# delta * u on GpSimd in three chunks, side additions one slot later, in_proj's input two blocks ahead, and the last image worked in parallel parts

## The chip, the cores and the metric

The kernel runs on one core of one Trainium2 chip. The time is device microseconds of one execution; the time before is the median of three executions. Engines are named as in the profile: PE (TensorE, matrix products and transposes), DVE (VectorE), ACT (ScalarE), POOL (GpSimd) and SP (SyncE, which here issues every DMA).

## The reference, cut to what matters

Four images of 64 x 64 positions and 96 channels pass a stack of layers. Layer 0 is a two-dimensional state-space block: a group norm, an input projection, a depthwise 3 x 3 convolution with SiLU, four selective scans (rows, columns, and both backwards), their merge, a layer norm, a gate and an output projection. Layer 1 is the same kind of block with 384 inner channels, between a real 2D Fourier transform and its inverse. Layers 2 and 3 are an attention without softmax, so that it can be done with small matrices, and a feed-forward part in quantised numbers. Everything but these quantised products is float32.

```python
def _selective_scan(u, dts, A, Bs, Cs, Dskip, delta_bias):
    delta = jax.nn.softplus(dts + delta_bias[None, :, :, None])
    ...
    def step(hst, inputs):
        ul, dl, bl, cl = inputs
        dA = jnp.exp(dl[..., None] * A)
        hst = hst * dA + (dl * ul)[..., None] * bl[:, :, None, :]
        y = jnp.einsum('bkdn,bkn->bkd', hst, cl)
        return (hst, y)
    ...
    return ys + Dskip[None, :, :, None] * u
...
x = x + _L0_conv_ref(_gn(x), ...)
x = _L1_conv_ref(x, ...)
t = _to_tokens(x)
t = t + _L2_attn_ref(_ln_t(t), ...)
t = t + _L2_ffn_ref(_ln_t(t), ...)
t = t + _L3_attn_ref(_ln_t(t), ...)
t = t + _L3_ffn_ref(_ln_t(t), ...)
```

The product `dl * ul` is the `du` of this document. The state has 16 entries for each channel.

## The kernel before, in words

**Three parts.** `build` first prepares image pair 0 alone (the head), then runs `scans` (the loop), then finishes image 3 alone (the tail). In head and tail a task owns the engines, with `wide=4` and eight PSUM buffers. In the loop the order on PE, DVE, ACT and POOL is written by hand and followed as it stands.

**The loop.** It has six phases: two image pairs of layer 0 (64 channels of both images side by side, three chunks of 128 partitions) and four images of layer 1. A phase is four directions, each cut into segments: eight of 512 positions in layer 0, and 512, 512, 384, 384 and 320 in layer 1. A segment is 12 steps: the state's entries in four groups `q` of four, and for each group the three channel chunks `c`. There are 144 segments and 1728 steps. A step on DVE is two scans `hx` (entries 4q and 4q+1), two scans `hy`, and the product `hcy` = hy * C. On POOL it is `hcx` = hx * C, a copy of the last state (`keep_state`, only where a segment isn't the last of its direction), and then, for the step that follows, `front_b`: two products hy = du * B. For `hx`, the input term comes from PE (transposes of `bx`) into PSUM instead. ACT makes the decays (`exp` in `front_x` and `front_y`) and `bx`; PE sums the products over the state in PSUM (`accumulate`). There is one buffer of `hy`: `front_b` of a step overwrites what `hcy` of the step before reads.

**The next segment.** While a segment is scanned, `prepare` makes what the next one needs, a piece at each slot: x_proj (`xpw`), dt (`dtw`), the softplus in one burst on ACT, `du` = delta * u (one DVE instruction over all three chunks, in a slot of the kind LATE), the load of u for the segment after (`load_u`, one buffer), and the transposed `dut`. At step 9 (`c == 0` of the last group) what is left of it is drained.

**Side work.** The other layers' work stands in lists of generators, one list for each phase. A step has three slots: after the two hx scans, after the first hy scan, and (LATE) ahead of `hcy`. At each, `prepare` advances, and a side task advances when a budget, `rate / 3` for each slot, has grown to one. A task's instructions up to its next `yield` are put there. `E.defer` holds an instruction until the next advance. All side work shares one PSUM buffer (`ms`). `E.require` runs a task to its end where a segment needs its result. The lists that matter here are `begin0` and `begin1` (norm or Fourier, in_proj by `visits`, convolution), `gate`, `end0` (`gated` with `out0`) and `end1` (`gated` with `out1`, then `inverse` and `tokens`).

**The tail** runs `end1` for image 3: `gated` (each block of up to 8 columns: the four directions' outputs and u are loaded by twos, summed by transposes on PE, normed with two products by `mean_w`, scaled, gated and projected), `inverse` (32 channels at a time) and `tokens` (layer norm over all 32 tiles in turn, the small products, attention group by group, norm, feed-forward group by group; two layers). Each of these runs as one stream.

Of the kernel before, what the change touches and what calls it, by code (L numbers as in the profile page):

```python
# [6 lines left out]
F32 = mybir.dt.float32  # L7
# [18 lines left out]
RATES = [1.75, 2.25, 2.35, 2.35, 2.35, 2.35]  # L26
# [97 lines left out]
class Block:  # L124
# [59 lines left out]
    def visits(self, E, sp, wi, xf, blocks, half, nm, w, done):  # L184


        def load(r, n):
            x = sp.tile([CH, 2, 512], F32, name=f"xi{half}_{nm}_{r}", tag=f"xin{w}", bufs=2)
            self.nc.sync.dma_start(out=x[:, :, : n * 64], in_=xf[:, :, r * 64 : (r + n) * 64])
            return x  # L190

        nxt = load(*blocks[0])
        yield
        yield
        for b, (r, n) in enumerate(blocks):
            x, nxt = nxt, load(*blocks[b + 1]) if b + 1 < len(blocks) else None
            pi = E.psum(f"pi{half}_{nm}_{r}")
            yield from self.in_proj(pi, wi, half, x, n * 64)
            E.defer(lambda r=r, n=n, pi=pi: done(r, n, pi))
            yield  # L200
# [149 lines left out]
    def gated(self, E, g, io, out_proj):  # L350


        nc, cfg = self.nc, self.cfg
        yn, yo = io["y"][cfg.nat], io["y"][1 - cfg.nat].rearrange("k (w r) c -> r w k c", r=cfg.NR)
        u, gz = io["u"][cfg.nat], io["gz"]
        with E.pool(f"{cfg.pre}nm{g}") as sp:
# [3 lines left out]
            tiles = [  # L360
                (b, i, r + i, min(2, n - i)) for b, (r, n) in enumerate(cfg.rows) for i in range(0, n, 2)
            ]

            def load(b, i, r, n):
                nm = f"{cfg.pre}_{g}_{r}"
                yt = sp.tile([P, 2, 2, C * P], F32, name=f"yt_{nm}", tag="yt", bufs=2)
# [5 lines left out]
                ut = sp.tile([P, C, P], F32, name=f"ut_{nm}", tag="ut", bufs=2)  # L372
# [3 lines left out]
            todo = iter(tiles)  # L376
            nxt = load(*next(todo))
            yield
            yield
            yield  # L380
            for b, (r, nr) in enumerate(cfg.rows):
                n = nr * 64
                nm = f"{cfg.pre}_{g}_{r}"
                z = sp.tile([P, C, 512], F32, name=f"zb_{nm}", tag="zb")
                nc.sync.dma_start(out=z[:, :, :n], in_=gz[:, :, r * 64 : r * 64 + n])
                y = sp.tile([P, C, 512], F32, name=f"yb_{nm}", tag="yb")
                for i in range(0, nr, 2):
                    m = min(2, nr - i) * 64
                    yt, ut = nxt
                    more = next(todo, None)  # L390
                    nxt = load(*more) if more else None
                    ps = E.psum(f"py_{nm}_{i}")[:, : C * P].rearrange("p (c t) -> p c t", c=C)
                    for c in range(C):
                        nc.tensor.matmul(
                            ps[:, c, :m], self.skip[:, c, :], ut[:, c, :m], start=(c == 0), stop=False
                        )
                    yield
                    for c in range(C):
                        for k in range(4):
                            nc.tensor.matmul(  # L400
                                ps[:, c, :m],
                                yt[:m, k // 2, k % 2, c * P : (c + 1) * P],
                                self.ident[:m, :m],
                                start=False,
                                stop=(c == C - 1 and k == 3),
                                is_transpose=True,
                            )
                        if c < C - 1:
                            yield
                    E.defer(lambda i=i, m=m, ps=ps, y=y: nc.scalar.copy(y[:, :, i * 64 : i * 64 + m], ps[:, :, :m]))  # L410
                    yield
                pm = E.psum(f"pm_{nm}")
                for c in range(C):
                    nc.tensor.matmul(pm[:, :n], self.mean_w, y[:, c, :n], start=(c == 0), stop=(c == C - 1))  # L414
                    yield
                for c in range(C):
                    nc.vector.tensor_tensor(y[:, c, :n], y[:, c, :n], pm[:, :n], ALU.subtract)
                yield
                sq = sp.tile([P, C, 512], F32, name=f"sq_{nm}", tag="sq")
                nc.scalar.activation(sq[:, :, :n], y[:, :, :n], AF.Square)  # L420
                yield
                pv = E.psum(f"pv_{nm}")
                for c in range(C):
                    nc.tensor.matmul(pv[:, :n], self.mean_w, sq[:, c, :n], start=(c == 0), stop=(c == C - 1))  # L424
                    yield
                ln = sp.tile([P, 512], F32, name=f"ln_{nm}", tag="ln")
                nc.scalar.activation(ln[:, :n], pv[:, :n], AF.Ln, bias=self.eps)
                nc.scalar.activation(pv[:, :n], ln[:, :n], AF.Exp, scale=-0.5)
                yield
                for c in range(C):  # L430
                    nc.vector.scalar_tensor_tensor(
                        y[:, c, :n], y[:, c, :n], self.lnw[:, c : c + 1], pv[:, :n], ALU.mult, ALU.mult
                    )
                yield LATE
                for c in range(C):
                    nc.vector.scalar_tensor_tensor(
                        y[:, c, :n], y[:, c, :n], self.lnb[:, c : c + 1], z[:, c, :n], ALU.add, ALU.mult
                    )
                yield
                yield from out_proj(E, sp, wo, y, r, nr)  # L440
# [9 lines left out]
class Seg:  # L450


    def __init__(self, ph, k, a, S, first, last):
# [8 lines left out]
        self.bx, self.b, self.c, self.u, self.after = {}, {}, {}, None, None  # L462

# [9 lines left out]
def scans(tc, ctx, phases, ident):  # L473
# [28 lines left out]
    def prepare(z):  # L502
# [35 lines left out]
        nc.scalar.preload_act_table_set(EXP_LN)  # L538
        yield
# [11 lines left out]
        yield LATE  # L551
        z.du = sp.tile([P, C, SM], F32, name=f"du_{nm}", tag="du", bufs=2)
        nc.vector.tensor_tensor(z.du[:, :, :S], z.delta[:, :, :S], u[:, :, :S], ALU.mult)
        if z.after and z.after.ph.needs[z.after.k % 2] in E.done:
            load_u(z.after)
        yield
        z.dut = sp.tile([P, NBK, C, P], F32, name=f"dut_{nm}", tag="dut", bufs=2)
        for c in range(C):
            pt = room().rearrange("p (b d) -> p b d", b=NBK)
# [3 lines left out]
            for lo, hi, n in z.runs:  # L563
                nc.scalar.copy(z.dut[:n, lo:hi, c], pt[:n, lo:hi, :])

# [46 lines left out]
    def drain(gen):  # L612
        for _ in gen:
            pass

# [97 lines left out]
    with tc.manual_schedule(engines=IN_ORDER):  # L713
        drain(prepare(segs[0]))
# [41 lines left out]
        for i, st in enumerate(steps):  # L756
            z, q, c, S = st.z, st.q, st.c, st.z.S
            nxt = steps[i + 1] if i + 1 < len(steps) else None
# [14 lines left out]
            if c == 0:  # L773
                if q + 1 < NQ:
                    fetch(z, q + 1)
                elif after:
                    drain(pgen)
# [21 lines left out]
            keep_state(nc.gpsimd.tensor_copy, st, hx, 4 * q)  # L799
            more.take(skip=long)  # L800
# [77 lines left out]
def out0(images, ins, x0):  # L878


    def task(E, blk, sp, wo, y, r, nr):
# [3 lines left out]
        for i, b in enumerate(images):  # L885
# [4 lines left out]
            for m in range(4):  # L890
# [8 lines left out]
                if m % 2:  # L899
                    yield  # L900
            nc.vector.tensor_tensor(xr, xr, po, ALU.add)
# [5 lines left out]
def out1(att, b):  # L907


    def task(E, blk, sp, wo, y, r, nr):  # L910
        nc = E.nc
        a = sp.tile([HH, 8, 2 * CH], F32, name=f"ab_{b}_{r}", tag="ab")
# [77 lines left out]
def inverse(E, cst, att, x, b, x1):  # L990
# [3 lines left out]
    G, HC, WP = 32, 16, 64  # L994
    xs, xd = (t.rearrange("(h w) c -> w h c", w=WW) for t in (x, x1))
    with E.pool(f"fi{b}") as sp:
# [5 lines left out]
        def load(c0):  # L1002
            a = sp.tile([2 * HH, WP, G], F32, name=f"at_{b}_{c0}", tag="at", bufs=2)
# [7 lines left out]
        nxt = load(0)  # L1011
        yield
        yield
        for c0 in range(0, CH, G):
            a, nxt = nxt, load(c0 + G) if c0 + G < CH else None
            v = sp.tile([2 * WP, G, HH], F32, name=f"v_{b}_{c0}", tag="v")
# [11 lines left out]
            for h0 in range(0, HH, 2 * HC):  # L1028
                xr = sp.tile([2 * WW, HC, G], F32, name=f"xr1_{b}_{c0}_{h0}", tag="xr", bufs=2)
# [11 lines left out]
                for p, h in halves:  # L1041
                    nc.sync.dma_start(out=xd[:, h, c0 : c0 + G], in_=xr[p])
        yield
# [5 lines left out]
def tokens(E, ins, consts, ident, x1, b, out):  # L1049


    nc = E.nc
    A = CH + 1
    with E.pool(f"tk{b}") as sp:
# [3 lines left out]
        nc.sync.dma_start(out=mask, in_=consts["head_mask"])  # L1058
        x = sp.tile([P, NT, CH], F32, name=f"tok_{b}", tag="tok")
        nc.sync.dma_start(out=x, in_=x1.rearrange("(p t) c -> p t c", t=NT))  # L1060
        xn = sp.tile([P, NT, A], F32, name=f"xn_{b}", tag="xn")
        nc.gpsimd.memset(xn[:, :, CH:A], 1.0)
        yield
        yield

        def layer_norm(nm):

            Q = 8
# [8 lines left out]
            for i in range(n + 2):  # L1077
# [3 lines left out]
                if i < n:  # L1081
                    t0 = i * Q
                    s = sp.tile([P, 2, Q], F32, name=f"lns_{nm}_{t0}", tag="lns", bufs=3)
# [13 lines left out]
                if i < n:  # L1097
                    sq = sp.tile([P, Q, CH], F32, name=f"lnq_{nm}_{t0}", tag="lnq", bufs=2)
# [6 lines left out]

        def small(rows, lhs, rhs, name, into):
# [4 lines left out]

        for ly in (2, 3):
            nm = f"{b}_{ly}"
            wq = sp.tile([A, 3 * CH], F32, name=f"wqkv_{nm}", tag="wqkv")
            nc.sync.dma_start(out=wq, in_=ins[f"l{ly}_wqkv"])
# [294 lines left out]
```

## Time and profile before

| what | us |
|---|---|
| median of three executions (11897.1 to 11918.08) | 11915.16 |
| profiled execution, its own time | 11917.7 |
| span of the profiled execution | 11915.9 |
| head, to the first scan | 220 |
| phases 0 and 1 (384 steps each) | 2587 and 2598 |
| phases 2, 3, 4, 5 (240 steps each) | 1479, 1473, 1559, 1538 |
| tail | 462 |

| stretch, us | PE busy | DVE busy | ACT busy | POOL busy |
|---|---|---|---|---|
| 220 to 2807 | 1966.8 | 2421.1 | 2171.7 | 2271.7 |
| 2807 to 5405 | 2086.8 | 2437.9 | 2173.7 | 2209.9 |
| 5405 to 6884 | 1240.5 | 1304.2 | 1104.7 | 1143.4 |
| 6884 to 8357 | 1229.6 | 1298.0 | 1120.2 | 1148.4 |
| 8357 to 9916 | 1220.2 | 1427.3 | 1180.1 | 1082.9 |
| 9916 to 11454 | 1196.4 | 1413.7 | 1154.9 | 1066.8 |
| 11454 to 11916 | 280.7 | 145.4 | 132.6 | 2.9 |

The page gives busy time of each engine over the span; the table by stretch gives it for a window. A line of the waits view names the engine and its line, what it waited for, the microseconds in total, how many times and the longest. A line of the timeline has the start, the length, the engine, the line of the kernel, the operation, the tiles and shapes, and in brackets the idle time ahead of it and what ended it. A wait is put down to what came last.

### The profile page before, as it was taken

Reading aid. Unit: us, or ns where it says so; the run is one execution under the profiler, and the core shown is the slowest. Engines: PE = TensorE matmul, PEld = TensorE weight load, DVE = VectorE, ACT = ScalarE, POOL = GpSimd, SP = SyncE. Lnnn points to the kernel's source line nnn. Section 1 sums busy time; section 2 is a strip of 40 time slices with the busy share of each in tenths; the row PEclk is TensorE's granted clock in tenths of the full one; section 3 lists DMA queues with packets and bytes.
Section 4 is the critical chain, followed back from the end, with each engine's and each line's share of the span. In section 5 each row is a group of like instructions: output and inputs, shape, how many; then the busy total and the mean of one; then the engine's idle time right before and its main releaser. Section 6 shows DMA issues by size and latency. Waiting matters only on the chain. (4 is left out here: it accounts for less than half of the span.)

```text
span 11915.9 us, 164932 instructions
## 1 busy us (share of the span) xinstructions
PE 9346.5 (78%) x54800; PEld 6707.9 (56%) x54800; DVE 10559.1 (89%) x10183; ACT 9087.2 (76%) x18534; POOL 8930.4 (75%) x7074
## 2 busy tenths in 40 slices
PE   6678777787788778777888888788778877887765
PEld 3455555555666556556665565565556555565544
DVE  6899999999998999998889988988989899899954
ACT  3678888898777888887768877777777777777733
POOL 2889999888877898987668878877668766686630
PEclk8789989989888989998889989898889888897886
DMA  5454444556555455455543443544234422442231
GB/s 142 119 139 119 121 125 112 141 161 161 148 145 118 124 132 136 126 133 162 149 123 118 132 127 113 155 134 117 82 96 149 112 90 85 143 129 88 83 106 35
DMA packets 1270448, 1469.07 MB, mean 123 GB/s; under 512 B 496024, under 2 KB 1033824, under 8 KB 1260120
## 3 DMA queue, kind: packets, MB, share of 16 engines
q1 hardware_dynamic: 1269591, 1458.53, 44.5%
q8 instruction: 430, 7.05, 0.3%
q14 instruction: 427, 3.49, 0.1%
HBM read 1221.74 MB, written 236.50 MB: 122 GB/s over the span
## 5 line engine op out<-in xcount | busy, mean ns | idle before, releaser
L646 POOL TENSOR_TENSOR hy_l<-du_l,bc_l 128x512 f32<-128x512 f32 (+2 forms) x3456 | 3957.2, 1166 | 2071.9 <-DVE hcy_l L815 1162.3
L798 POOL TENSOR_TENSOR hcx_l<-hx_l,bc_l 128x1024 f32<-128x1024 f32 (+2 forms) x1616 | 3524.4, 2181 | 254.3 <-DVE hx_l L653 218.3
L593 ACT ACTIVATE bx_l<-dut_l,bt_l 128x192 f32<-128x192 f32 (+2 forms) x6272 | 2792.8, 498 | 0.0
L675 PE MATMUL acc_l<-ident,hcx_l 128*128 128x128 f32 (+1 forms) x12000 | 1845.4, 301 | 392.8 <-POOL hcx_l L798 387.7
L628 ACT ACTIVATE ax_l<-delta_l,l_alog 128x512 f32<-128x512 f32 (+2 forms) x3456 | 2139.3, 667 | 0.0
L675 PE MATMUL acc_l<-ident,hcy_l 128*128 128x128 f32 (+1 forms) x11994 | 1830.5, 300 | 349.6 <-DVE hcy_l L815 345.6
L675 PEld LDWEIGHTS acc_l<-ident,hcy_l 128*128 128x128 f32 (+1 forms) x11994 | 1533.7, 154 | 911.2 <-DVE hcy_l L815 523.0
L675 PEld LDWEIGHTS acc_l<-ident,hcx_l 128*128 128x128 f32 (+1 forms) x12000 | 1505.6, 154 | 885.6 <-POOL hcx_l L798 667.9
L815 DVE TENSOR_TENSOR hcy_l<-hy_l,bc_l 128x1024 f32<-128x1024 f32 (+2 forms) x1615 | 1955.2, 1211 | 43.0
L653 DVE TENSOR_TENSOR_SCAN hx_l<-ax_l,state_l,b_l 128x512 f32<-128x512 f32 (+2 forms) x1648 | 1785.8, 1124 | 209.9 <-PE b_l L623 153.8
L653 DVE TENSOR_TENSOR_SCAN hy_l<-b_l,state_l,hy_l 128x512 f32<-128x512 f32 (+2 forms) x1648 | 1782.0, 1119 | 80.5 <-ACT b_l L628 73.3
L628 ACT ACTIVATE b_l<-delta_l,l_alog 128x512 f32<-128x512 f32 (+2 forms) x1912 | 1196.4, 628 | 742.2 <-DVE hx_l L653 707.9
L623 PE MATMUL b_l<-ident,bx_l 128*128 128x128 f32 (+1 forms) x6718 | 1178.2, 303 | 389.7 <-DVE hy_l L653 197.9
L628 ACT ACTIVATE ab_l<-delta_l,l_alog 128x512 f32<-128x512 f32 x1321 | 906.8, 689 | 599.6 <-DVE hx_l L653 550.9
L623 PEld LDWEIGHTS b_l<-ident,bx_l 128*128 128x128 f32 (+1 forms) x6718 | 826.8, 153 | 875.2 <-DVE hy_l L653 320.7
L653 DVE TENSOR_TENSOR_SCAN hx_l<-ax_l,state_l,ab_l 128x512 f32<-128x512 f32 x962 | 1176.8, 1264 | 78.9 <-PE ab_l L623 54.8
L653 DVE TENSOR_TENSOR_SCAN hy_l<-ab_l,state_l,hy_l 128x512 f32<-128x512 f32 x961 | 1172.1, 1257 | 62.7 <-POOL hy_l L646 33.9
L623 PE MATMUL ab_l<-ident,bx_l 128*128 128x128 f32 x5288 | 878.0, 301 | 414.5 <-DVE hy_l L653 227.4
L666 POOL COPY state_l<-hx_l 128x2 f32<-128x2 f32 x1344 | 1140.2, 848 | 0.0
L623 PEld LDWEIGHTS ab_l<-ident,bx_l 128*128 128x128 f32 x5288 | 640.9, 152 | 745.3 <-DVE hy_l L653 339.3
L272 PE MATMUL pc_l<-pad_l,l_dg 128*128 128x512 f32 (+2 forms) x1656 | 791.9, 566 | 69.9 <-ACT uh_l L250 63.9
L176 PE MATMUL pi_l<-xi_l,l_wi 96*128 96x384 f32 (+6 forms) x912 | 466.5, 626 | 246.7 <-DMA xi_l<-xn 94.7
(193 smaller groups left out, 11940.5 us busy)
## 6 DMA issues: line engine op xcount, KB each, us to landing
bc_l<-l_xd_l SPq DMA_DIRECT2D x1536, 256.0 KB
bc_l<-l_xd_l SPq DMA_DIRECT2D x384, 512.0 KB
bc_l<-l_xd_l SPq DMA_DIRECT2D x384, 384.0 KB
us_l<-l_u SPq DMA_DIRECT2D x96, 768.0 KB
l_y<-y_l SPq DMA_DIRECT2D x288, 256.0 KB
bc_l<-l_xd_l SPq DMA_DIRECT2D x192, 320.0 KB
yt_l<-l_y SPq DMA_DIRECT2D x264, 192.0 KB
yt_l<-l_y SPq DMA_DIRECT2D x128, 384.0 KB
```

The source lines that it names most:

```text
L176: self.nc.tensor.matmul(out[i * cfg.PI : (i + 1) * cfg.PI, :n], wi[:, ki, half, :], xin[:, max(i, ki), :n], start=(ki == 0), stop=(ki == c ...
L272: nc.tensor.matmul(pc[:, : n * 64].rearrange("p (r w) -> p r w", w=64), diag[:, t, :], pad[:, r - p0 + dy : r - p0 + dy + n, dx : dx + 64] ...
L593: nc.scalar.activation(t[:n, b, :, ch], z.dut[:n, b, :, ch], AF.Copy, scale=z.bt[:n, b, m : m + 1])
L623: nc.tensor.transpose(pb[:, t : t + n], st.z.bx[st.q, j][:n, b, st.c], ident[:n, :n])
L628: nc.scalar.activation(out, z.delta[:, st.c, : z.S], AF.Exp, scale=z.blk.A[:, st.c, z.k, n : n + 1])
L646: nc.gpsimd.tensor_tensor(st.hy[:, j, :S], st.z.du[:, st.c, :S], st.z.b[st.q][:, j, :S], ALU.mult)
L653: nc.vector.tensor_tensor_scan(h[:, j, : z.S][:, ::step], a[:, : z.S][:, ::step], b[:, : z.S][:, ::step], 0.0 if z.first else z.state[st.c ...
L666: copy(z.state[st.c][:, n0 : n0 + 2].rearrange("p (j o) -> p j o", o=1), h[:, :, e : e + 1])
L675: nc.tensor.matmul(z.acc[st.c][:n, b, :], hc[:, j, t : t + n], ident, start=(n0 + j == 0 and b == 0), stop=(n0 + j == NST - 1 and b == 0), ...
L798: nc.gpsimd.tensor_tensor(hcx[:, :, :S], hx[:, :, :S], z.c[q][0][:, :, :S], ALU.mult)
L815: nc.vector.tensor_tensor(hcy[:, :, :S], st.hy[:, :, :S], z.c[q][1][:, :, :S], ALU.mult)
```

## The change

`du` leaves DVE: `make_du` issues one POOL product for each channel chunk, at most one in a step, behind that step's `hcx` and state copy, from the step after the softplus on; `dut`'s transposes follow chunk by chunk. `load_u` comes behind the third chunk. In the side work, `gated` gets a yield between the product with `mean_w` and the subtraction, `out0` one ahead of its addition, the token tasks (`attend`, `feed`) one more ahead of theirs. `visits` loads two blocks ahead with three buffers. `tokens` loads weights ahead of its input. The rates rise from 2.25 and 2.35 to 2.35 and 2.5. Where a task owns the engines, `gated` runs as three workers over the blocks, `inverse` as three over the channels, and `tokens` in four parts of 8 tiles, with both layers' weights loaded ahead of the inverse; the result is stored in parts. In the loop (`W == 1`) these tasks stay one stream.

```diff
-RATES = [1.75, 2.25, 2.35, 2.35, 2.35, 2.35]
+RATES = [1.75, 2.35, 2.5, 2.5, 2.5, 2.5]
...
-            x = sp.tile([CH, 2, 512], F32, name=f"xi{half}_{nm}_{r}", tag=f"xin{w}", bufs=2)
+            x = sp.tile([CH, 2, 512], F32, name=f"xi{half}_{nm}_{r}", tag=f"xin{w}", bufs=3)
...
-        nxt = load(*blocks[0])
+        ahead = [load(*blk) for blk in blocks[:2]]
+        yield
         yield
         yield
         for b, (r, n) in enumerate(blocks):
-            x, nxt = nxt, load(*blocks[b + 1]) if b + 1 < len(blocks) else None
+            ahead += [load(*blk) for blk in blocks[b + 2 : b + 3]]
+            x = ahead.pop(0)
...
+        W = min(E.wide, 3)
...
+            def worker(w):
+
+                blocks = list(enumerate(cfg.rows))[w::W]
...
                     for c in range(C):
+                        nc.tensor.matmul(pm[:, :n], self.mean_w, y[:, c, :n], start=(c == 0), stop=(c == C - 1))
+                        yield
+                    yield
+                    for c in range(C):
+                        nc.vector.tensor_tensor(y[:, c, :n], y[:, c, :n], pm[:, :n], ALU.subtract)
...
+            yield from together([worker(w) for w in range(W)], W)
...
         nc.scalar.activation(z.delta[:, :, :S], z.delta[:, :, :S], AF.Softplus)
         nc.scalar.preload_act_table_set(EXP_LN)
+        z.ready = now
...
-        yield LATE
-        z.du = sp.tile([P, C, SM], F32, name=f"du_{nm}", tag="du", bufs=2)
-        nc.vector.tensor_tensor(z.du[:, :, :S], z.delta[:, :, :S], u[:, :, :S], ALU.mult)
-        if z.after and z.after.ph.needs[z.after.k % 2] in E.done:
-            load_u(z.after)
-        yield
         z.dut = sp.tile([P, NBK, C, P], F32, name=f"dut_{nm}", tag="dut", bufs=2)
         for c in range(C):
+            while z.made <= c:
+                yield
             pt = room().rearrange("p (b d) -> p b d", b=NBK)
...
+    def make_du(z):
+
+        if z.made == 0:
+            z.du = sp.tile([P, C, SM], F32, name=f"du_{z.nm}", tag="du", bufs=2)
+        c, z.made = z.made, z.made + 1
+        nc.gpsimd.tensor_tensor(z.du[:, c, : z.S], z.delta[:, c, : z.S], z.u[:, c, : z.S], ALU.mult)
+        if z.made == C and z.after and z.after.ph.needs[z.after.k % 2] in E.done:
+            load_u(z.after)
...
             nc.gpsimd.tensor_tensor(hcx[:, :, :S], hx[:, :, :S], z.c[q][0][:, :, :S], ALU.mult)
             keep_state(nc.gpsimd.tensor_copy, st, hx, 4 * q)
+            if after and after.ready is not None and after.ready < now and after.made < C:
+                make_du(after)
             more.take(skip=long)
...
                 if m % 2:
                     yield
+            yield
             nc.vector.tensor_tensor(xr, xr, po, ALU.add)
...
+        if W > 1:
+            loads = [load(c0) for c0 in range(0, CH, G)]
+            yield from together([channels(w * G, a, w) for w, a in enumerate(loads)], W)
...
+        def part(ly, p, wo, q):
+            nm, w = f"{b}_{ly}", p % W
+            groups = range(p * Q // 4, (p + 1) * Q // 4)
+            for g in groups:
+                yield from attend(nm, g, w, wo)
+            yield from layer_norm(nm + "f", p)
+            for g in groups:
+                yield from feed(nm, g, w, q)
+            if ly == 2:
+                yield from layer_norm(f"{b}_3a", p)
+            else:
+                t = slice(p * Q, (p + 1) * Q)
+                nc.sync.dma_start(out=out[b].rearrange("(p t) c -> p t c", t=NT)[:, t], in_=x[:, t])
...
+            if W > 1:
+                yield from together([part(ly, p, wo, q) for p in parts], W)
+                continue
...
+            rest = tokens(E, ins, consts, ident, x1[b], b, out)
+            if E.wide > 1:
+                yield next(rest)
             yield from inverse(E, consts, att, x0[b], b, x1[b])
-            yield from tokens(E, ins, consts, ident, x1[b], b, out)
+            yield from rest
```

## The prediction, made before the changed kernel had run

> **What bounds the kernel now.** I read the busy times of the page first, then the table by stretch, then the waits of VectorE (DVE) and GpSimd (POOL) inside the scan loop, and last the timeline of single scan steps.
>
> ```profile
> PE 9346.5 (78%) x54800; PEld 6707.9 (56%) x54800; DVE 10559.1 (89%) x10183; ACT 9087.2 (76%) x18534; POOL 8930.4 (75%) x7074
> ```
>
> The span has three parts: a head of 220 us, the scan loop to 11454 (1728 steps in six phases), and a tail of 462 us in which image 3 is finished alone. In the loop's phases 0 and 1 (220 to 5405, two image pairs of layer 0) DVE is busy 94% and POOL 88 and 85%; in phases 2 to 5 DVE has 88 to 92% and POOL 69 to 78%. So DVE looks like the bound. The timeline of DVE, and then that of POOL, over three steps of phase 0 show that POOL is nearly one too:
>
> ```profile
> 1506.15 2.43 DVE L653 TENSOR_TENSOR_SCAN hy_l<-ab_l,state_l,hy_l 128x512 f32<-128x512 f32 x2
> 1508.50 2.25 DVE L553 TENSOR_TENSOR du_l<-delta_l,us_l 128x1536 f32<-128x1536 f32 x1
> 1510.67 1.62 DVE L815 TENSOR_TENSOR hcy_l<-hy_l,bc_l 128x1024 f32<-128x1024 f32 x1
> ...
> 1514.59 2.42 DVE L653 TENSOR_TENSOR_SCAN hy_l<-ab_l,state_l,hy_l 128x512 f32<-128x512 f32 x2
> 1517.05 1.24 DVE L815 TENSOR_TENSOR hcy_l<-hy_l,bc_l 128x1024 f32<-128x1024 f32 x1
> ...
> 1523.03 1.29 DVE L815 TENSOR_TENSOR hcy_l<-hy_l,bc_l 128x1024 f32<-128x1024 f32 x1
> ```
> ```profile
> 1518.42 2.51 POOL L646 TENSOR_TENSOR hy_l<-du_l,bc_l 128x512 f32<-128x512 f32 x2 [1.21 <-issue]
> 1520.88 2.37 POOL L798 TENSOR_TENSOR hcx_l<-hx_l,bc_l 128x1024 f32<-128x1024 f32 x1
> 1524.47 2.51 POOL L646 TENSOR_TENSOR hy_l<-du_l,bc_l 128x512 f32<-128x512 f32 x2 [1.23 <-DVE hcy_l L815]
> ```
>
> Seen here: a step without side work lasts 6.05 us (1518.42 to 1524.47 on POOL). POOL works 4.83 of it and stands for the 1.22 of hcy, because front_b may not overwrite hy before hcy has read it. DVE is full too (4.86 of scans, 1.2 of hcy). Both engines are at their limit at once. The step with du is 2.2 us longer.
>
> **What the Trainium skill says.** SBUF — State Buffer, section "SBUF: two separate sides": the port pair that VectorE and GpSimd share is an exclusive lock for a whole instruction, also against a VectorE operation with two SBUF inputs. The trace agrees: hcy (hy and bc, both in SBUF) takes 1.24 us alone and 1.62 or more where it starts while POOL still works, and POOL's two-element state copy has a median of 1177 ns beside a shortest of 175. du on VectorE is such an operation as well. GPSIMD Engine Reference, section 3.1: a tensor_tensor of 2048 elements takes 1.96 times as long on GpSimd; here 2363 ns (hcx, 1024) against 1225 (median of hcy), 1.93 times. TensorE: Matmul & The Clock Gate, "What's actually happening": the array gets half its clock until it has been busy for a while; the last 218 us show a mean clock of 0.55.
>
> **Part 1, du to GpSimd.** Removed from DVE: 96 x 1.962 + 32 x 1.567 + 16 x 1.280 us = 259 us (groups of L553 by form). Added to POOL: 288 chunks of 512, 96 of 384, 48 of 320; by the rows of front_b's same shapes 1.272, 0.999 and 0.863 us, so 504 us. The order of the two programs shows the place: before, du stands in step 7 of each 12-step segment ahead of hcy; after, one chunk stands in each of steps 6, 7 and 8, behind hcx and the state copy, ahead of the next front_b. Behind it in POOL's queue is front_b, which step n+1's hy scans need; the reload of u on SP's queue waits for the third chunk (step 8 instead of 7, needed at step 12, so hidden: four steps are 25 us); the transposes of du on PE and the copies of dut on ACT wait for each chunk.
> With a 0.18 us state copy a side-free step is 6.23 on POOL; with a chunk of 1.25 it is 7.48. The mean steps of phases 0 and 1 are 2587/384 = 6.74 and 2598/384 = 6.77, so a chunk isn't covered there. I took the trace's steps 6, 7, 8 from hcy's end to hcy's end, took du off step 7, and stretched each step that was then shorter than its POOL instructions + an undisturbed hcy (1.222, 0.950, 0.820 by shape) + the chunk, less 0.2 us by which neighbouring POOL records overlap. Sums over all segments: step 6 +112, step 7 -80, step 8 +136, so +168 us (phases 0 and 1 +128, 2 and 3 +36, 4 and 5 +4). With an overlap of 0.3 it is +135. I take **+150**. Bounds: -259 if POOL's stretch hides wholly behind side work; +400 if moreover each chunk delays PE's transposes and ACT's copies by half a microsecond that DVE feels (432 x 0.5 = 216).
>
> **Part 2, side work one slot later, loads two ahead.** Waits of DVE in the loop:
>
> ```profile
> DVE xr L901 <- PE po L892: 90.3, 30, 9.2
> ...
> DVE tok L1165 <- PE pao L1163: 46.3, 31, 3.9
> DVE y L1202 <- ACT y L1200: 27.4, 22, 3.7
> DVE qw L1129 <- DMA w<-in_l_w: 26.0, 3, 10.1
> DVE yb_l L417 <- PE pm_l L414: 25.8, 18, 4.0
> ```
>
> Columns: microseconds in total, times, the longest. DVE stands in these, its scans queue behind, and POOL waits for hcy. Each of the five gets another yield (the weights' casts come behind a longer lead), about 2.6 us (a 6.5 us step over 2.5 side steps), against mean waits of 3.0, 1.5, 1.2, 8.7 and 1.4. Together 216 us. In phase 0 PE waits 49 us for xi in eight places; the DVE gaps of more than 1 us that stand behind these sum to 43. With a second load under way and a third buffer they should mostly go. I take four fifths of 216 + 43: **-200**. At the least -60 (the wait returns as PE backlog or POOL is the limit), at most -260.
> The rates rise only because there are more yields: 3397 side steps in the loop for 3199, and every phase's list still ends inside its phase (the last at step 1727 for 1722), so no list is forced through. Cost nothing; if one were forced, its remaining steps would stand on the path.
>
> **Part 3, the tail.** Before, one stream with one buffer of y, sq and z:
>
> ```profile
> 11454.00:11650.00 196.00, 124.16 (x580) 91.41 (x580) 26.41 (x46) 28.41 (x50) 1.78 (x2) 0.79 0.43 111
> 11650.00:11698.00 48.00, 35.04 (x408) 26.08 (x408) 4.14 (x7) 7.04 (x12) 1.08 (x2) 0.86 0.82 101
> 11698.00:11916.00 218.00, 121.53 (x640) 88.20 (x640) 114.87 (x208) 97.18 (x262) 0.00 (x0) 0.55 0.06 20
> ```
>
> Columns: length, busy PE, PEld, DVE, ACT, POOL, clock, DMA share, GB/s. Gated norm: three workers overlap; the floor is PE's 124 or DMA's 0.43 x 196 = 84 us of full use, at the 0.8 share that its best stretch has 105; with 12 us ahead of the first matmul and a last block's chain I take 145, -51. Inverse: DMA already has 0.82, so 42, -6. Tokens: no engine has over 122 of 218; four parts overlap, two full stops remain (pg and the small products), the weights no longer follow the load of tok (18 us before the first norm): 150, -68. Sum **-125**, between -60 and -180. The in-order queues could let one worker's DMA wait stop all, hence the lower end.
>
> **Part 4**, head and first segment: 3 first chunks cost 3.8 instead of 2.0 us, xi's extra lead gives some back. Zero.
>
> **Sum.** 11917.7 (the profiled execution; its span is 11915.9) + 150 - 200 - 125 = 11743. The median shown is 2.5 lower, so **11740**.
>
> **Rivals.**
> *POOL takes the chunks for nothing.* For it: POOL idles 1162 us for hcy in the loop. Against it: that idling is the lock and the single hy buffer. If two thirds hold, du is -100 instead of +150: 11490.
> *Slower: GpSimd becomes the bound.* Place: steps 6 to 8, front_b behind the chunk, hcy behind the lock, PE's du transposes and ACT's dut copies behind both. For it: in phases 0 and 1, 94 and 92% of the time is POOL's own work or hcy's lock; against it: later phases have 0.6 us of slack a step. At du +400 and half of part 2 lost to the same limit: 11917.7 + 400 - 100 - 125 = 12090. It decides, with half of part 2 lost, from du +250 on.
> *The transfers gain nothing and only the tail counts*: du +150, sides -60, tail -125: 11880.
> *Not done as said*: the order shows all chunks, loads and workers in place; no chance given.
>
> **Chances.** The sum's case 0.56 (its own range 11640 to 11850), POOL for nothing 0.19, only the tail 0.08, slower 0.17. A measurement of this kernel can tell 0.2%, 24 us, from no change. Nearly all of the first three is faster, their upper edges reach no change: faster 0.76, same 0.06, slower 0.18. Eight in ten: **11500 to 11950**.
>
> **What would show it.** In the profile after: no L553 group on DVE, a POOL group of du with 432 instructions near 1.17 us mean; in phases 0 and 1 step 7 about 7.5 to 8 instead of 8.6 and 8.0 (means of the trace), steps 6 and 8 near 7.5 instead of 6.3 to 6.8; phase 0 longer by some 30 us (+69 - 35), phases 2, 4, 5 shorter; more "DVE hy <- POOL hy"; xr, tok, yb waits under a third; tail near 337. Wrong if phase 0 and 1 shrink by over 50 us each (chunks are hidden), if DVE's wait for POOL passes 300 us, or if the tail stays over 400.

## The result, and the profile after

The changed kernel takes 11804.01 us (median of four executions, 11795.96 to 11825.49) against 11906.49 us for the kernel before beside it: ratio 0.9916, interval [0.9899, 0.9934]. It is faster by some 100 us; the forecast was 11740, within 11500 to 11950. Its profiled execution has a span of 11798.2 us against 11915.9.

| stretch | before, us | after, us | difference |
|---|---|---|---|
| head | 220.8 | 212.7 | -8 |
| phase 0 | 2586.3 | 2599.7 | +13 |
| phase 1 | 2597.7 | 2593.4 | -4 |
| phase 2 | 1479.4 | 1478.4 | -1 |
| phase 3 | 1472.6 | 1455.5 | -17 |
| phase 4 | 1558.8 | 1534.0 | -25 |
| phase 5 | 1538.0 | 1524.0 | -14 |
| tail | 462.3 | 400.5 | -62 |

The busy times of the page of the changed kernel:

```profile
PE 9242.9 (78%) x54800; PEld 6731.3 (57%) x54800; DVE 10551.5 (89%) x10039; ACT 9082.5 (77%) x18533; POOL 9395.9 (80%) x7507
```

DVE lost 144 instructions of 259 us in all, and its busy time went from 10559.1 to 10551.5 only. The group of hcy shows where about two thirds of the difference are: in the kernel before, L815 stands for 1955.2 us at a mean of 1211 ns. The rest is in no single group.

Groups of the kernel after (line, tiles, forms, count; busy us, mean ns; idle time ahead):

```profile
L841 DVE TENSOR_TENSOR hcy_l<-hy_l,bc_l 128x1024 f32<-128x1024 f32 (+2 forms) x1611 | 2117.1, 1314 | 47.5
...
L577 POOL TENSOR_TENSOR du_l<-delta_l,us_l 128x512 f32<-128x512 f32 (+2 forms) x432 | 553.2, 1281 | 64.4 <-ACT delta_l L546 64.4
```

hcy grew by 162 us, and the chunks are recorded at 553 us instead of the 504 that front_b's rows gave. The timeline of DVE and POOL in two steps with a chunk shows why (phase 0 of the kernel after, in a segment that is the last of its direction and so has no state copies; lines of other engines left out):

```profile
1497.03 2.37 POOL L822 TENSOR_TENSOR hcx_l<-hx_l,bc_l 128x1024 f32<-128x1024 f32 x1
...
1498.87 1.61 DVE L841 TENSOR_TENSOR hcy_l<-hy_l,bc_l 128x1024 f32<-128x1024 f32 x1
1499.35 2.27 POOL L577 TENSOR_TENSOR du_l<-delta_l,us_l 128x512 f32<-128x512 f32 x1
...
1500.40 2.44 DVE L676 TENSOR_TENSOR_SCAN hx_l<-ax_l,state_l,ab_l 128x512 f32<-128x512 f32 x2
1501.55 0.63 POOL L306 COPY ut_l<-uh_l 128x256 f32<-128x256 f32 x1
...
1502.13 2.52 POOL L669 TENSOR_TENSOR hy_l<-du_l,bc_l 128x512 f32<-128x512 f32 x2
1503.45 2.51 DVE L676 TENSOR_TENSOR_SCAN hy_l<-ab_l,state_l,hy_l 128x512 f32<-128x512 f32 x2 [0.62 <-POOL hy_l L669]
1504.59 2.37 POOL L822 TENSOR_TENSOR hcx_l<-hx_l,bc_l 128x1024 f32<-128x1024 f32 x1
...
1506.00 2.04 DVE L841 TENSOR_TENSOR hcy_l<-hy_l,bc_l 128x1024 f32<-128x1024 f32 x1
```

The chunk starts at 1499.35, while hcy holds until 1500.48, and is recorded with 2.27 us: about 1.13 us of that is hcy's, the rest its own work. A copy of the side work (`ut`, 0.63 us) follows, and only then comes front_b, so DVE has done its hx scans at 1502.84 and stands 0.62 us for hy. In the next step hcy starts at 1506.00, but hcx runs to 1506.96: hcy is recorded with 2.04 us. From one front_b to the next (1502.13 to the next chunk step's 1509.69 in the same view) it is 7.56 us, such a copy included, and POOL has no idle time in it.

Most chunks stand in segments with state copies (seven of eight segments in phases 0 and 1, four of five later). There the copy takes the wait for hcy and the chunk is recorded alone (phase 0, other engines and scans left out):

```profile
1110.48 2.51 POOL L669 TENSOR_TENSOR hy_l<-du_l,bc_l 128x512 f32<-128x512 f32 x2
...
1112.95 2.36 POOL L822 TENSOR_TENSOR hcx_l<-hx_l,bc_l 128x1024 f32<-128x1024 f32 x1
1114.34 2.05 DVE L841 TENSOR_TENSOR hcy_l<-hy_l,bc_l 128x1024 f32<-128x1024 f32 x1
1115.25 1.19 POOL L689 COPY state_l<-hx_l 128x2 f32<-128x2 f32 x1
1116.40 1.26 POOL L577 TENSOR_TENSOR du_l<-delta_l,us_l 128x512 f32<-128x512 f32 x1
...
1117.62 2.50 POOL L669 TENSOR_TENSOR hy_l<-du_l,bc_l 128x512 f32<-128x512 f32 x2
```

This step is 7.14 us from front_b to front_b. In phases 0 and 1 there are 121 that hold just such a state copy and a chunk between hcx and front_b; their median is 7.15 us, without idle time of POOL. With the state copy alone the median is 6.14 us (6.15 in the kernel before). So a chunk makes such a step 1.0 us longer.

Waits of DVE in the loop, kernel after (us in total, times, longest), against those of before in the prediction:

```profile
DVE hy_l L676 <- POOL hy_l L669: 79.5, 78, 10.7
...
DVE hx_l L676 <- POOL hy_l L669: 30.2, 20, 2.8
DVE yb_l L435 <- ACT pv_l L432: 30.0, 22, 4.5
...
DVE xr L928 <- PE po L918: 16.4, 11, 3.8
...
DVE tok L1212 <- PE pao L1209: 12.2, 15, 2.7
```

xr fell from 90.3 to 16.4 us and tok from 46.3 to 12.2; the wait for `pm` in the gated norm is under 4 us, and the next one of the same block, for `pv`, rose from 16.9 to 30.0. The wait for ScalarE's `y` in the feed-forward part fell from 27.4 to 16.9 only. DVE's waits for POOL's hy rose from 54 to 110 us (43.4 + 11.0 before).

### The profile page after: what moved, and what is told of

Read it like the earlier page. It is cut to its first block, busy times and chain, and to the rows that moved or that the text cites. A ratio compares the mean times of both kernels' runs of the same rounds, so it can differ in the third digit from the quotient of the medians.

```text
span 11798.2 us, 165545 instructions
## 1 busy us (share of the span) xinstructions
PE 9242.9 (78%) x54800; PEld 6731.3 (57%) x54800; DVE 10551.5 (89%) x10039; ACT 9082.5 (77%) x18533; POOL 9395.9 (80%) x7507
## 5 line engine op out<-in xcount | busy, mean ns | idle before, releaser
L841 DVE TENSOR_TENSOR hcy_l<-hy_l,bc_l 128x1024 f32<-128x1024 f32 (+2 forms) x1611 | 2117.1, 1314 | 47.5
L698 PE MATMUL acc_l<-ident,hcx_l 128*128 128x128 f32 (+1 forms) x11976 | 1883.8, 306 | 351.9 <-POOL hcx_l L822 348.2
L698 PEld LDWEIGHTS acc_l<-ident,hcx_l 128*128 128x128 f32 (+1 forms) x11976 | 1549.9, 157 | 792.4 <-POOL hcx_l L822 581.5
L646 PE MATMUL b_l<-ident,bx_l 128*128 128x128 f32 (+1 forms) x6694 | 1124.4, 297 | 298.5 <-DVE hy_l L676 173.8
L689 POOL COPY state_l<-hx_l 128x2 f32<-128x2 f32 x1344 | 1091.3, 812 | 0.0
L274 PE MATMUL pc_l<-pad_l,l_dg 128*128 128x512 f32 (+2 forms) x1656 | 800.8, 572 | 34.3 <-ACT uh_l L252 26.4
L567 PE MATMUL pp_l<-ident,du_l 128*128 128x128 f32 (+1 forms) x1584 | 326.1, 336 | 534.9 <-POOL du_l L577 503.3
```

Of the source, the lines that this page charges most:

```text
L274: nc.tensor.matmul(pc[:, : n * 64].rearrange("p (r w) -> p r w", w=64), diag[:, t, :], pad[:, r - p0 + dy : r - p0 + dy + n, dx : dx + 64] ...
L567: nc.tensor.transpose(pt[:n, i, :], z.du[:, c, t : t + n], ident)
L646: nc.tensor.transpose(pb[:, t : t + n], st.z.bx[st.q, j][:n, b, st.c], ident[:n, :n])
L689: copy(z.state[st.c][:, n0 : n0 + 2].rearrange("p (j o) -> p j o", o=1), h[:, :, e : e + 1])
L698: nc.tensor.matmul(z.acc[st.c][:n, b, :], hc[:, j, t : t + n], ident, start=(n0 + j == 0 and b == 0), stop=(n0 + j == NST - 1 and b == 0), ...
L841: nc.vector.tensor_tensor(hcy[:, :, :S], st.hy[:, :, :S], z.c[q][1][:, :, :S], ALU.mult)
```

## The experiments

Differences between two kernels are taken between their ratios to the kernel before, times 11906 us, since each group of runs has its own runs of the kernel before. A ratio is known to about 0.0013 on either side, that of the changed kernel to 0.0018, so a difference to about 22 us, or 26 us against the changed kernel.

**1. Each part undone, and du alone.** du back on DVE:

```diff
+        z.du = sp.tile([P, C, SM], F32, name=f"du_{nm}", tag="du", bufs=2)
+        nc.vector.tensor_tensor(z.du[:, :, :S], z.delta[:, :, :S], u[:, :, :S], ALU.mult)
...
-            if after and after.ready is not None and after.ready < now and after.made < C:
-                make_du(after)
```

> The changed kernel with du back on VectorE: one instruction over the three chunks in step 7, as before; everything else as changed. Theory A (GpSimd and the lock are the limit, moving du cost time): faster than the changed kernel's 11804, by +150 as predicted, so 11655; by what the steps of the two traces show (sum over steps 7, 8 and 9: -149, +137, +77 us) by 65 us, so 11740. Theory B (GpSimd takes the chunks behind its waits, the 259 us off VectorE are what brought the gain): slower, 11900 to 12000.

Measured: 11716.22 us, ratio 0.9831 [0.9819, 0.9843]: faster than the changed kernel by 101 us. The opposite edit, `make_du` alone put into the kernel before:

> The kernel before with du alone moved to GpSimd in three chunks; rates, side work and tail as before. Theory A: slower than 11906, by 65 to 150 us, so 11970 to 12055. Theory B: faster, 11650 to 11800. If the loss here is larger than the gain from undoing du in the changed kernel, the two parts share a limit.

Measured: 12053.02 us, ratio 1.0118 [1.0105, 1.0132], so du on POOL costs 140 us by itself. The extra slots of the side work taken out (with rates that end the lists within their phases):

```diff
-RATES = [1.75, 2.35, 2.5, 2.5, 2.5, 2.5]
+RATES = [1.75, 2.3, 2.4, 2.4, 2.4, 2.4]
...
-            yield
+            if W > 1:
+                yield
...
```

> The changed kernel without the extra yields ahead of the side additions in the loop (gated, out0, attend, feed), with rates 2.3 and 2.4 so that every list still ends inside its phase; du on GpSimd, loads two ahead and the tail as changed. Theory A (the waits of VectorE on xr, tok, y and yb were on the path, 190 us of them before): slower than 11804 by 100 to 160 us, so 11905 to 11965. Theory B (VectorE waits at another place for the same engines): within 30 us of 11804.

Measured: 11956.07 us, ratio 1.0039 [1.0026, 1.0052]: the slots are worth 146 us where the rest of the change stands. The tail as one stream again:

```diff
-        def alone(ctx, task, arg):
+        def alone(ctx, task, arg, wide=4):
...
-            alone(tail, end1, 3).finish()
+            alone(tail, end1, 3, 1).finish()
```

> The changed kernel with image 3 worked as one stream, as before. Theory A: slower by what the traces show, 462 against 401 us in the tail, so by 60, 11865. Theory B (a part of the tail's saving is given back by the loop's end, since the last store of image 2 now runs at the last step): by less than 40, under 11845.

Measured: 11887.75 us, ratio 0.9982 [0.9973, 0.999]: 79 us. The tail of this run's trace is 474 us long, against 462 in the kernel before and 400.5 in the changed one. in_proj's input one block ahead again:

```diff
-tag=f"xin{w}", bufs=3)
+tag=f"xin{w}", bufs=2)
...
-        ahead = [load(*blk) for blk in blocks[:2]]
-        yield
+        ahead = [load(*blk) for blk in blocks[:1]]
...
-            ahead += [load(*blk) for blk in blocks[b + 2 : b + 3]]
+            ahead += [load(*blk) for blk in blocks[b + 1 : b + 2]]
```

> The changed kernel with in_proj's input one block ahead again (two buffers, one yield less). The prediction took four fifths of 43 us for this: 11804 + 34 = 11838 us. Theory D, from two runs so far (loop of the kernel before with du moved, 11358 us, less that of the changed kernel without the extra slots, 11342): +17 us, 11821. Rival: nothing, 11804.

Measured: 11873.92 us, ratio 0.9972 [0.9962, 0.9982]: 67 us, above all that was expected. Waits of PE, and then of DVE, of this kernel in the loop:

```profile
PE pi_l L176 <- DMA xi_l<-xf: 61.1, 21, 7.3
...
PE pi_l L176 <- DMA xi_l<-xn: 22.9, 6, 7.3
```
```profile
DVE xr L927 <- PE po L917: 43.2, 16, 5.1
```

In the changed kernel these are 16.3, 12.2 and 16.4 us. But `po` is not late because PE has just stood for xi: none of the 16 waits for xr has a wait of PE for xi in the 4 us ahead of it. The larger part of the 67 us is ahead of DVE's scans, whose waits from the first step on sum to 683 us here and to 632 in the changed kernel; what links them to the loads is open. Undone one at a time, slots and input cost 146 and 67 us; undone together (du alone against the tail as one stream, 1.0118 - 0.9982) they cost 162. So they do not simply add up, as far as three such differences can tell.

**2. The price of du in either place.** From the kernel with du on DVE the product is left out:

```diff
-        z.du = sp.tile([P, C, SM], F32, name=f"du_{nm}", tag="du", bufs=2)
-        nc.vector.tensor_tensor(z.du[:, :, :S], z.delta[:, :, :S], u[:, :, :S], ALU.mult)
+        z.du = z.delta
```

> This is the changed kernel with du back on VectorE (11716 us) and then the product left out: delta itself takes the place of du, so the result is not the reference's. It gives the floor from which both places of du are priced. Theory A (the side of SBUF that VectorE and GpSimd share is full, so whatever is taken off it comes off the time, above all in phases 0 and 1): 259 us of VectorE work go and 200 to 259 us of time with them, 11460 to 11515 us. du on VectorE then costs about its own length, and du on GpSimd that plus 88. Rival B (du on VectorE lies mostly beside waits for PE and for DMA): under 130 us, 11590 us or more.

Measured: 11537.99 us, ratio 0.9691 [0.9678, 0.9705]. So du costs 167 us on DVE (0.9831 - 0.9691) and 268 us on POOL (0.9916 - 0.9691). That lies between the two theories: of DVE's 258 us two thirds are on the path, of POOL's 504 us a little over half. POOL does hide a larger share, but its instruction takes twice as long, and 53% of 504 is more than 65% of 258. The groups of the two kernels with du on DVE and on POOL agree: with du on DVE, hcy is back at its old mean.

Groups of the kernel with du on DVE (the changed kernel's are above):

```profile
L843 DVE TENSOR_TENSOR hcy_l<-hy_l,bc_l 128x1024 f32<-128x1024 f32 (+2 forms) x1616 | 1950.0, 1207 | 43.6
...
L563 DVE TENSOR_TENSOR du_l<-delta_l,us_l 128x1536 f32<-128x1536 f32 (+2 forms) x144 | 257.8, 1790 | 36.7 <-ACT delta_l L546 36.7
```

Of the 258 us that leave DVE, 167 come back in hcy's record (2117.1 - 1950.0); that this is also the price of du on DVE is chance.

**3. How a chunk costs: its place and the waits behind it.** Each chunk behind the next step's front_b:

```diff
             if nxt:
                 front_b(nxt)
+            if after and after.ready is not None and after.ready < now and after.made < C:
+                make_du(after)
```

> The changed kernel with each chunk issued behind the next step's front_b instead of ahead of it. Theory A (capacity: the chunk's 1.1 us plus hcy's and the copies' turns fill the step wherever the chunk stands): phases 0 and 1 unchanged within 15 us each, 11785 to 11815 us in all. Rival C (order: what costs is that front_b, and so the hy scans, come a chunk later): most of the 88 us come back, 11720 to 11740 us, and VectorE's waits for POOL's hy fall back to about 43 us. In between (phases 2 to 5 gain some 30 us, phases 0 and 1 nothing): 11770.

Measured: 12116.35 us, ratio 1.0177 [1.0163, 1.0191]: 311 us slower, against both theories. Taken from the end of one hcy to the end of the next, by place in the 12-step segment, place 9 alone took 265 us more than in the changed kernel, over all segments, and place 7 another 55. The timeline of that place, phase 0 (lines left out marked):

```profile
1538.43 1.25 DVE L676 TENSOR_TENSOR_SCAN hy_l<-ab_l,state_l,hy_l 128x512 f32<-128x512 f32 x1
1539.42 1.26 POOL L577 TENSOR_TENSOR du_l<-delta_l,us_l 128x512 f32<-128x512 f32 x1
...
1540.74 1.12 PE L567 MATMUL pp_l<-ident,du_l 128*128 128x128 f32 x4 [2.75 <-POOL du_l L577]
...
1541.89 0.59 ACT L570 COPY dut_l<-pp_l 128x512 f32<-128x512 f32 x1 [6.75 <-PE pp_l L567]
1542.38 0.70 ACT L651 ACTIVATE ab_l<-delta_l,l_alog 128x512 f32<-128x512 f32 x1
...
1543.17 1.28 DVE L676 TENSOR_TENSOR_SCAN hy_l<-ab_l,state_l,hy_l 128x512 f32<-128x512 f32 x1 [3.49 <-ACT ab_l L651]
```

The third chunk ends at 1540.68. At step 9 what is left of `prepare` is drained, so the transposes of that chunk stand in PE's queue and the copy of dut in ACT's, ahead of the exp that the next hy scan needs. PE waits 2.75, ACT 6.75 and DVE 3.49 us for one chunk. To see how much of this chain stands in the changed kernel, PE was given delta to transpose instead of du, in both orders:

```diff
-                nc.tensor.transpose(pt[:n, i, :], z.du[:, c, t : t + n], ident)
+                nc.tensor.transpose(pt[:n, i, :], z.delta[:, c, t : t + n], ident)
```

> The changed kernel, all three chunks computed on GpSimd as before, but PE transposes delta instead of du, so that neither PE nor ScalarE waits for GpSimd's chunks; dut then holds another value than the reference asks for. It parts the two ways in which a chunk can cost. Theory H (the cost is GpSimd's own time and VectorE's hcy behind the shared side of SBUF): 11785 to 11805 us, since in the changed kernel PE's and ScalarE's waits for chunks lie beside VectorE's own wait for hy. Rival I (the waiting chain chunk, transpose, dut copy, exp costs VectorE time): 11720 to 11765 us.

> The kernel with each chunk behind front_b (12116 us, 312 above the changed kernel), with PE transposing delta instead of du as in the run beside it, so no PE or ScalarE wait for a chunk. Theory I': that order was slow because the third chunk now ended after the forced rest of the segment's preparation had been put in PE's and ScalarE's queues, ahead of the next step's exps (VectorE's waits for ScalarE's b and ab were 363 us against 120): without the chain it takes 11770 to 11830 us, as the order then makes little difference. Rival (the order costs GpSimd and VectorE themselves, because hcx and so hcy come a chunk later): 12000 us or more.

Measured: 11783.35 us (0.9894 [0.988, 0.9908]) in the changed kernel's order, 26 us less than with the wait and no more than can be told from nothing; 11920.33 us (1.0013 [1.0005, 1.0021]) behind front_b, 195 us less. So the chain costs little where the change put the chunks, though PE stands 503 us in it (285 times). The trace of the changed kernel shows where these waits lie: only 17 us of them fall into idle time of DVE, which is in its scans and hcy meanwhile. Behind front_b the chain is the larger part of the 311 us. With the chain gone from both orders, the later place still costs 142 us (1.0013 - 0.9894), between the two theories. That stays open: no run separates hcx and hcy coming a chunk later from the last transposes still being put out in the drain.

The second and the third chunk in one step:

```diff
                 make_du(after)
+                if after.made == 2:
+                    make_du(after)
```

> The changed kernel with the second and the third chunk both in the second of the three steps, so that the third is done a step ahead of the forced rest of the preparation. Theory H (GpSimd's time alone): 11795 to 11815 us, the cost only moves from place 9 to place 8 of the segment. Rival I (the third chunk's wait chain in place 9 costs): some 40 us less, 11765 us. A third outcome: two chunks in a row delay hy by 2.3 us in a step that has no slack and lose more than they save, 11830 us or more.

Measured: 11814.66 us, ratio 0.9921 [0.9909, 0.9933], no difference from the changed kernel that can be told. Place 8 rose by 103 us and place 9 fell by 98 against it: the cost moved and kept its size, as it does when what counts is the time that POOL is taken.

**4. The tail.** With du on DVE, inverse's loads ahead of the tokens' weights in SP's queue, once with the token parts of a layer starting six slots apart (an edit to `together`, not shown), once with them in step:

```diff
+        if W > 1:
+            yield
...
+            back = inverse(E, consts, att, x0[b], b, x1[b])
             if E.wide > 1:
                 yield next(rest)
-            yield from inverse(E, consts, att, x0[b], b, x1[b])
+                yield next(back)
+                yield next(rest)
+            yield from back
             yield from rest
```

> The changed kernel with du on VectorE (11716 us), with two edits in the tail: inverse's loads go to SP's queue ahead of the tokens' 16 weight loads, and the four token parts of a layer start six slots apart instead of together. Theory E (the tail fell short for these two reasons): inverse ends about 20 us earlier, and the two layers take 62 to 68 us each instead of 82, so 11650 to 11660 us. Rival F (the parts are bound by an engine's work whatever their phase, or the shift only adds a ramp): only the 20 us, 11696. Rival G (the ramp of three shifts costs more than the overlap gives): 11716 or more.

> The best version so far (the changed kernel with du on VectorE, 11716 us) with inverse's loads ahead of the tokens' weight loads in SP's queue and the token parts in step as in the changed kernel. The run with both tail edits showed the stretch from gated norm's last product to inverse's last add shorter by 12 us, and the token stretch longer by 9. Theory: 11704 us, and faster than both kernels by over 90 us. Rival (the weights then come late and the tokens wait for them): 11716 us or more.

Measured: 11709.7 us (0.9839 [0.9825, 0.9852]) with the shift, 11691.1 us (0.982 [0.9806, 0.9834]) without. Against the changed kernel with du on DVE (0.9831) the first is 10 us slower and the second 13 us faster, less than the ratios can tell, so the reading goes by the traces. The table by stretch of the kernel with du on DVE, and then of the one with the loads moved and no shift (length; busy PE, PEld, DVE, ACT, POOL; clock, DMA share, GB/s), for gated norm, inverse with the first norm's load, and the two token layers:

```profile
11319.00:11473.00 154.00, 108.51 (x592) 85.92 (x592) 28.97 (x53) 28.40 (x51) 2.12 (x4) 0.82 0.67 150
11473.00:11550.00 77.00, 36.83 (x408) 26.51 (x408) 6.37 (x18) 7.04 (x12) 0.61 (x1) 0.72 0.65 102
11550.00:11633.00 83.00, 46.08 (x320) 34.91 (x320) 56.48 (x104) 47.11 (x132) 0.00 (x0) 0.69 0.00 1
11633.00:11714.00 81.00, 46.42 (x320) 35.08 (x320) 50.64 (x93) 46.98 (x131) 0.00 (x0) 0.67 0.05 20
```
```profile
11302.00:11457.00 155.00, 108.78 (x584) 86.06 (x584) 26.61 (x49) 28.37 (x51) 1.49 (x3) 0.82 0.67 148
11457.00:11522.00 65.00, 36.98 (x408) 26.65 (x408) 6.59 (x18) 7.03 (x12) 1.23 (x2) 0.76 0.76 123
11522.00:11606.00 84.00, 46.16 (x320) 34.83 (x320) 56.71 (x104) 47.50 (x132) 0.00 (x0) 0.66 0.00 1
11606.00:11686.00 80.00, 46.29 (x320) 35.10 (x320) 50.43 (x93) 46.53 (x131) 0.00 (x0) 0.69 0.05 20
```

The second stretch is 12 us shorter, with DMA at 0.76 instead of 0.65, and the others are the same within 1 us. PE's first wait there for the input (`at`) is 26.4 us with the weights ahead and 10.1 with them behind (9.9 in the run with the shift): the weights did stand ahead of the loads. With the shift the two layers took 84 and 91 us, so a shift of six slots does not shorten them. The last version, at 0.982 of the kernel before, is the fastest of those that compute what the reference asks for; against the changed kernel du on DVE gives nearly all of it.

## Why the prediction was right in sign and high in the gain

The parts can be added in the order in which the runs allow it. du alone is +140 us. From there to the changed kernel it is -241 (1.0118 to 0.9916), of which the tail takes 79; the slots and the input two ahead take the other 162. The sign came out since these two outweigh du's loss, as the sum had it.

| part | predicted, us | measured, us |
|---|---|---|
| du to POOL | +150 | +140 alone, +101 beside the rest |
| slots and input two ahead | -200 | -162 |
| tail | -125 | -79 (in the traces -62) |
| sum | -175 | -101 |

**du: right in sign and size, and by the mechanism named.** The steps with a chunk are full on POOL, without idle time, as the prediction said. The usual one takes 7.15 us. The prediction had 7.48 for it, less the 0.2 to 0.3 us that its sum takes off for overlapping records, so 7.18 to 7.28. The 7.56 us of the first timeline are no confirmation of the 7.48: there is a side copy in them and no state copy. The trace after agrees with what the Trainium skill says in SBUF — State Buffer, section "SBUF: two separate sides", on the lock of a whole instruction: the chunk is recorded with 2.27 us where it meets hcy and hcy with 2.04 where it meets hcx, against 1.26 and 1.22 alone. The run with du on DVE, 101 us faster than the changed kernel, rules out the rival *POOL takes the chunks for nothing*: du on DVE does cost 167 us there, but on POOL it costs more. How much of POOL's price is the lock and how much only POOL's full queue, no run separates. *GpSimd becomes the bound* had the right place, but needed +250 from du; DVE's waits for POOL's hy are 110 us, not over 300.

Wrong in it: the places. Chunk and hcy were put in the order chunk, hcy; in phases 0 and 1 hcy goes first for 163 of 192 chunks, and the chunk delays the step after. From hcy's end to hcy's end, the prediction had +112, -80 and +136 us for steps 6, 7 and 8 (168 in sum). In the run with du alone the places 6, 7, 8 and 9 changed by +25, -118, +144 and +80 (131 in sum), so the sum came out near, though not its places. In phases 0 and 1 of the changed kernel step 7 takes 7.67 and 7.46 us, about as forecast, steps 8 and 9 take 7.15 to 7.74, and step 6 stays at 6.71 and 6.34. The chain over PE and ACT, which the prediction held at half a microsecond a chunk for its upper bound (216 us), measured 26 us in the changed kernel, not told from nothing, with an order near by in which it costs 195.

**Slots and input: right but high.** Four fifths of 259 us were taken. Four of the five waits did go nearly as named (xr, tok, the weights and yb for `pm`: from 188 to 33 us); y fell only from 27.4 to 16.9, and yb's wait for `pv` rose. To see what a microsecond of wait is worth, du has to stay in one place. From the run with du alone to the changed kernel, DVE's waits in the side work of the loop fell from 315 to 126 us, and those ahead of its scans, from the first step on, rose from 608 to 632. That is 165 us less waiting in these two traces, whose loops differ by 173 us; by the ratios it is 162 us less time. So a microsecond of wait was worth about one of time. The 200 of the prediction are 35 us above this, and 24 of these are the waits that came back ahead of the scans. From the kernel before to the changed one the waits ahead of the scans rose from 533 to 632, and the run with du alone has 608: most of that rise is du's.

**Tail: the largest miss, in two terms.** With the borders at gated norm's last product and inverse's last addition, before is 192, 47 and 222 us long, after is 156, 68 and 177:

| stretch | predicted change, us | measured, us |
|---|---|---|
| gated norm | -51 | -37 |
| inverse | -6 | +20 |
| tokens | -68 | -45 |

The inverse was costed by its DMA share of 0.82 without the 16 weight loads that the change puts ahead of it in SP's queue. Twelve of the 26 us that it missed came back when the loads changed places; the other 14 stay open. For gated norm a DMA share of 0.8 was expected and 0.64 was reached. The tokens' two layers take 82 us each with no engine busy for more than 57 of them; which chain holds them is open; a shift of the parts did not help. The prediction called itself wrong if the tail stays over 400: it is 400.5.

**The rest.** The profile has no du on DVE, 432 chunks on POOL (1281 ns, not 1170; 45 of them are recorded with more than 1.6 us, where the wait for hcy is included), phase 0 longer by 13 us, phases 4 and 5 shorter and phase 2 the same, xr and tok under a third. The head gave 8 us where zero was taken.

## What to carry to other kernels

An instruction that two engines can run is not priced by how full each engine is, if they share a port: here du cost 167 us on the engine that is 89% busy and 268 on the one that is 75% busy, where its instructions take twice as long. A wait of a full engine can be worth a slot of distance: here, together with the earlier loads, 189 us of such waits went, 24 came back at another place, and the time fell by 162. In a queue in program order, look at what has been put behind the piece that is moved: the same chunk behind two more instructions cost 311 us more.

## What the runs showed of the hardware

The profile's busy time includes the wait of one engine for the other: a chunk of 512 is recorded with 1.26 us where it meets no hcy and 2.27 where it does, a state copy of two elements with 1.19 behind hcy and 0.18 alone, and hcy with 1.22 alone, 2.04 where it meets hcx, and 2.82 once (at 1533.33 us in the run with the chunks behind front_b). So DVE lost 259 us of instructions here and stayed as busy as before, and its busy share near 90% does not say how much of it is work.
